# Sliding-window attention: turning the probabilities by VectorE's block transposes and a trip through DRAM, with a unit's scores moved forward

## The chip, the cores and the metric

The kernel runs on one core of a Trainium2 chip, as one launch. The metric is the device time of that launch in microseconds (us), the median of several runs. Everything is in float32. The core has five engines that work side by side, each through its own queue in order: TensorE (PE, matrix products; PEld is its loading of weights), VectorE (DVE), ScalarE (ACT), GpSimd (POOL) and SyncE (SP), which here only issues DMAs. Engines wait for each other by semaphores.

## The reference

1024 tokens (4 sequences of 256) of 512 features go through three residual steps: `x = x + 0.5 * ffn(layernorm(x))`, `x = x + attn(layernorm(x))`, and the first step again. `ffn` is a base product of 512x512 with a routed low-rank part (8 experts of rank 16, the two best for each token). `attn` is the part that the change touches:

```python
q = (x @ wq).reshape(B, S, 32, 128)        # 32 query heads
k = (x @ wk).reshape(B, S, 8, 128)         # 8 key/value heads, 4 query heads share one
v = (x @ wv).reshape(B, S, 8, 128)
q, k = rope(q, pos), rope(k, pos)
scores = einsum(qg, k) * 128 ** -0.5
allowed = (j <= i) & (j > i - 128)         # a window of 128 keys
attn = softmax(where(allowed, scores, neg))
out = einsum(attn, v) @ wo
```

## The kernel before, in words

Tokens are handled in two halves of 512 (two sequences each). After the first `ffn`, attention runs over 16 **groups**, one for each half `h` and key/value head `g`; `n` in the code is the number of a group, 1 to 16. A group has two **units**, one for each sequence `b`; there are 32 units.

The big products (queries, keys, values, output) use a 2x2 scheme with seven instead of eight block products, so many sums and differences of weights and activations run on GpSimd: `sum_weights` (wqs, wks, wvs), `sum_o_weights` (wos, four operations, each from the one before), and the sums of `outputs` (oTs). A group's `queries` are seven products, numbered in the code; after products 2, 5, 4 and 3 VectorE applies `rope` (one operation L484 and two L486 each, and an addition before it for 5, 4 and 3) and GpSimd adds the two parts into `qT` (L492).

A unit's attention is worked in blocks of 32 query positions (BLK), with four query heads side by side on the 128 partitions (32 positions x 4 heads). Queries of the first half of a sequence (4 blocks) see keys of the first half only; those of the second half see a window that spans both. The steps of a unit are:

- `scores` (L684): eight products on TensorE into PSUM (sa: the first four blocks; sb: the other four, two banks); VectorE adds the mask and takes maxima for sa (L696), and for sb puts the two ends of each window in place with a predicated copy (L714) and takes the maxima (L716).
- `exponentials` (L720): two small VectorE operations scale the maxima (L722, L723); ScalarE makes eight exponentials with their sums (L729) into `probs`, a single buffer for all units.
- `normalize` (L734): reciprocal on VectorE (L735), two multiplications of 128x512 on GpSimd (L738).
- `transposes` (L742): TensorE turns each of the eight 128x128 blocks of `probs` (L746), ScalarE copies the first four out of PSUM (L750), VectorE multiplies the other four by the masks `old` and `new` (L755), which split a window by the half that its keys are in.
- `values` (L761): one product oa for the first half, two that add up in ob (old keys, new keys), and two copies by ScalarE to `oT` (L771).
- `outputs` (L777): four sums on GpSimd and a list `late` of four steps, the output products y in the order (4), (1,6), (2,3), (7,5). They are not run at once but strewn between the next unit's work by `run(late, ...)`. The first, (4), reads the last of the four sums wos.

The order on TensorE, VectorE, ScalarE and GpSimd is the order of the program (`manual_schedule`), up to the last three units, where a scheduler orders TensorE and VectorE. In a group's first unit a string gives the order. Its letters are the query products 1 to 7, `y` a late output step, `n` normalize, `t` turn, `w` sum_o_weights, and some steps that only certain groups have (`k` `v` in the first group; `c` `d` `e` differences of tokens in group 7; `a` work of the last ffn near the end):

```python
order = {0: "1n6kv2754t3", 4: "1yn6a27cy5d4yte3yw"}[len(late)]
```

After it come the scores of the second unit, the values of the first, and the start of the next group's keys (odd `n`) or values (even `n`). The second unit runs the rest of those products, late steps, its own transposes, the scores of the next group's first unit, and its values. PSUM has four banks for products and four for scores and transposes. All DMAs are issued by SP, in one queue; the weights of a later group are loaded ahead.

Of the kernel before, what the change touches and what calls it, by code (L numbers as in the profile page):

```python
# [38 lines left out]
def macaron_kernel(  # L39
# [17 lines left out]
    const = ctx.enter_context(tc.tile_pool(name="const", bufs=1))  # L57
    sb = ctx.enter_context(tc.tile_pool(name="sb", bufs=2))
    ps = ctx.enter_context(tc.tile_pool(name="ps", bufs=2, space=bass.MemoryType.PSUM))

    def mm_bank(name):
        return ps.tile([P, 512], F32, tag="mm", bufs=4, name=name)
# [23 lines left out]
    nc.sync.dma_start(out=cos_sb, in_=cos[:, :S])  # L86
    sin_sb = const.tile([HD, S], F32, name="sin_sb")
    nc.sync.dma_start(out=sin_sb, in_=sin[:, :S])

    weights = {}  # L90

# [118 lines left out]
        return bass.AP(tensor=w.tensor, offset=w.offset, ap=[w.ap[0], [-BLK, 2], w.ap[2]])  # L210


    probs = const.tile([P, 2 * NB, P], F32, name="probs")
    for e in range(NB - 1):
        nc.gpsimd.memset(probs[:, e, (e + 1) * BLK :], 0.0)


    old = const.tile([P, NB, BLK], F32, name="old")
# [405 lines left out]
    def project_values(h, g):  # L624


        x, w = xs[h], weights["vs", h, g]
        dst = sb.tile([P, TPH, 2 * HD], F32, tag="v", name=f"v_{h}_{g}")
        vS[h, g] = dst
        banks = [mm_bank(f"v{n}_{h}_{g}").rearrange("p (b i f) -> p b i f", b=BPH, i=2) for n in range(2)]  # L630
        (c11, c12), (c21, c22) = ((bank[:, 0], bank[:, 1]) for bank in banks)
        (v11, v12), (v21, v22) = (
            (dst[:, :2, cols], dst[:, 2:, cols]) for cols in (slice(0, HD), slice(HD, 2 * HD))
        )
        p1c, u2, v1 = (
            temp(n, f"v_{h}_{g}")[:, :S].rearrange("p (i f) -> p i f", i=2) for n in ("p1c", "u2", "v1")
        )

        def product(n, bank, start=False):
            for i in range(2):  # L640
                for c in range(2):
                    nc.tensor.matmul(  # L642
                        bank[:, i, :], x[n - 1][:, c, ts(i, P)], w[n - 1][:, c, :],
                        start=(start and i == 0 and c == 0), stop=(c == 1), skip_group_check=True,
                    )

        def first():
            product(1, c11, True)
            nc.scalar.copy(p1c, c11)
            product(6, c22, True)  # L650

        def both():
            add(u2, c22, p1c)

        def second():
            product(5, c12)
            add(v1, c12, u2)
            product(7, c21)
            add(v22, c21, v1)

        def others():
            product(2, c11)
            product(4, c21)
            add(v21, c21, u2)
            product(3, c12)
            nc.scalar.copy(v11, c11)
            add(v12, c12, u2)

        return first, both, second, others

# [10 lines left out]
        nc.scalar.copy(vS[h, g][:, i, :], pv[:, : 2 * HD])  # L681


    def scores(h, g, b):  # L684
        o = b * S
        q, k = qT[h, g][:, b], kT[h, g]
# [7 lines left out]
        for e in range(NB):  # L694
            n = (e + 1) * BLK
            nc.vector.tensor_tensor_reduce(  # L696
                pr[:, e, :n], pa[:, e, :n], mask[:, P - n :], SM_SCALE, -3.4e38,
                ALU.add, ALU.max, mx[:, e : e + 1],
            )
        pairs = []  # L700
        for p in range(NB // 2):
            pb = score_bank(f"sb_{h}_{g}_{b}_{p}")
            for r in range(2):

                m = 2 * p + r
                at = r * P + m * BLK
                nc.tensor.matmul(  # L707
                    pb[:, at : at + P + BLK], q[:, NB + m],
                    k[:, o + m * BLK : o + m * BLK + P + BLK], start=True, stop=True,
                )  # L710
            w = picked(p)
            n = w.shape[-1]
            pb = pb.rearrange("p (r k) -> p r k", k=P)
            nc.vector.copy_predicated(pb[:, :2, :n], w, pb[:, 1:3, :n])  # L714
            pb = pb[:, :2, :]
            nc.vector.tensor_reduce(mx[:, NB + 2 * p : NB + 2 * p + 2], pb, AX.X, ALU.max)  # L716
            pairs.append(pb)
        return pr, mx, sm, pairs, f"{h}_{g}_{b}"

    def exponentials(pr, mx, sm, pairs, name):  # L720
        nm = sb.tile([P, 2 * NB], F32, tag="nm", bufs=3, name=f"nm_{name}")
        nc.vector.tensor_scalar(nm[:, :NB], mx[:, :NB], -1.0, None, ALU.mult)  # L722
        nc.vector.tensor_scalar(nm[:, NB:], mx[:, NB:], -SM_SCALE, None, ALU.mult)  # L723
        for n in range(2 * NB):
            keys_of = min(n + 1, NB) * BLK
            src, scale = (
                (pr[:, n, :], 1.0) if n < NB else (pairs[(n - NB) // 2][:, n % 2, :], SM_SCALE)
            )
            nc.scalar.activation(  # L729
                pr[:, n, :keys_of], src[:, :keys_of], AF.Exp, bias=nm[:, n : n + 1], scale=scale,  # L730
                accum_out=sm[:, n : n + 1],
            )

    def normalize(pr, sm):  # L734
        nc.vector.reciprocal(sm, sm)  # L735
        for n in range(0, 2 * NB, NB):
            w = pr[:, n : n + NB, :]
            nc.gpsimd.tensor_tensor(  # L738
                w, w, sm[:, n : n + NB].unsqueeze(2).to_broadcast([P, NB, P]), ALU.mult
            )  # L740

    def transposes(h, g, b, pr):  # L742
        def turn(n0, name):
            pt = ps.tile([P, NB, G, BLK], F32, tag="s", bufs=4, name=f"{name}_{h}_{g}_{b}")
            for e in range(NB):
                nc.tensor.transpose(pt[:, e, :, :], pr[:, n0 + e, :], ident)  # L746
            return pt

        p0 = sb.tile([P, NB, G, BLK], F32, tag="p0", bufs=1, name=f"p0_{h}_{g}_{b}")
        nc.scalar.copy(p0, turn(0, "t0"))  # L750
        pt = turn(NB, "t1")
        parts = []
        for n, w in enumerate((old, new)):
            part = sb.tile([P, NB, G, BLK], F32, tag=f"p1{n}", bufs=1, name=f"p1{n}_{h}_{g}_{b}")
            nc.vector.tensor_tensor(  # L755
                part, pt, w.unsqueeze(2).to_broadcast([P, NB, G, BLK]), ALU.mult
            )
            parts.append(part)
        return p0, parts

    def values(h, g, b, p0, p1):  # L761
        oT = sb.tile([HD, G, S], F32, tag="oT", bufs=4, name=f"oT_{h}_{g}_{b}")
        v = vS[h, g - g % 2]
        cols = ts(g % 2, HD)
        for i, parts in enumerate(([p0], p1)):
            po = mm_bank(f"o{'ab'[i]}_{h}_{g}_{b}")
            for n, part in enumerate(parts):
                nc.tensor.matmul(  # L768
                    po, v[:, 2 * b + n, cols], part, start=(n == 0), stop=(n == len(parts) - 1)
                )  # L770
            nc.scalar.copy(  # L771
                oT[:, :, ts(i, P)].rearrange("p j (e q) -> p e j q", e=NB),
                po.rearrange("p (e j q) -> p e j q", e=NB, j=G),
            )
        return oT

    def outputs(h, g, b, oT):  # L777
# [179 lines left out]
    last = units[-1]  # L957
    ahead = scores(*units[0])
    exponentials(*ahead)
    for u, (h, g, b) in enumerate(units):  # L960
        n = groups.index((h, g)) + 1
        left = len(units) - u
        if left == 3:
            in_order.close()
        if left < 4:
            normalize(ahead[0], ahead[2])
        fill(left, 0)
        if left == 1:
            nc.scalar.activation(root, eps, AF.Sqrt)
        parts = []  # L970

        def turn(at=(h, g, b), pr=ahead[0]):
            parts.extend(transposes(*at, pr))

        if b == 0 and n < len(groups):

            order = {0: "1n6kv2754t3", 4: "1yn6a27cy5d4yte3yw"}[len(late)]
            steps = queries(*groups[n], nc.vector.tensor_copy, ends)  # L980
            steps |= {
                "y": lambda: run(late, 1), "n": lambda: normalize(ahead[0], ahead[2]),
                "w": lambda: sum_o_weights(h, g), "v": lambda: project_v(0, 0, 2),
                "k": lambda: sum_weights("k", *groups[2]), "a": lambda: fill(left, 1),
                "t": turn, "c": None, "d": None, "e": None,
            }

            if g == NKV - 2 and h + 1 < NHALF:
# [6 lines left out]
        elif b == 1 and n + 1 < len(groups):  # L995
# [3 lines left out]
            if g == NKV - 2 and h + 1 < NHALF:  # L999
                more_tokens[4]()  # L1000
            second()
            normalize(ahead[0], ahead[2])
            if n == 2:
                for t in behind:
                    measure(t, "a")
            if n % 2 == 1 and (h, g) != groups[NKV]:
                sum_weights("v", *groups[n + 1])
            others()
            fill(left, 4)
            turned = [behind.popleft() for _ in range(2 if behind and n in (4, 6) else 0)]  # L1010
            for t in turned:
                scale(t, "a")
            if n % 2 == 0 and n + 2 < len(groups):
                sum_weights("k", *groups[n + 2])
# [2 lines left out]
            elif n % 2 == 0 and n + 2 < len(groups):  # L1017
                load_v(*groups[n + 2])
            run(late, len(late) - 1)
            for t in turned:  # L1020
                norm_attn(t, scaled=True)
        else:
            run(late, len(late))
            fill(left, 1)
        if b == 1 and n + 1 < len(groups):
# [12 lines left out]
        if b == 0 and 1 < n < len(groups):  # L1038
            load_o(*groups[n])
        if not parts:  # L1040
            turn()
        fill(left, 2)
        run(late, len(late) - 1)
        if left > 1:
            ahead = scores(*units[u + 1])

        combine = late.popleft() if g == NKV - 1 and b == 1 and left > 1 else None
# [3 lines left out]
        if u == 0:  # L1051
            project_v(0, 0, 3)
            load_v(*groups[2])
        oT = values(h, g, b, *parts)
        if b == 0 and n + 1 < len(groups):

            first, *begun = keys(*groups[n + 1]) if n % 2 == 1 else project_values(*groups[n])
            first()
        if left > 1:
            exponentials(*ahead)  # L1060
            if combine:
                combine()
            late.extend(outputs(h, g, b, oT))
# [73 lines left out]
```

## Time and profile before

| | |
|---|---|
| time, median of 3 runs | 765.95 us (765.70 to 766.31) |
| span of the profiled execution, first to last instruction | 764.3 us |
| mean granted TensorE clock | 0.999 of full speed |
| busy share of the span: PE, POOL, DVE, ACT | 99%, 71%, 73%, 28% |
| DMA, share of 16 engines | 18.7% |

The profile is of one execution; for that execution the page gives the span, and the times are those of the three runs, so what lies around the span is taken as the difference of the median and the span, 1.65 us. In a row of the timeline the first number is the start in us from the start of the span, the second the time from the first instruction's start to the last one's end; then engine, line, operation, output <- inputs, shapes, and how many instructions; brackets hold the idle time before it and what ended it. Products of 128x256 show up as two instructions each. Products overlap, so the price of a step on TensorE is the distance from its start to the start of what follows.

### The profile page before, as it was taken

The page shows a single profiled execution, that of the slowest core. Times are in us where ns is not written, and L with a number is a line of the kernel's source. Part 1 is how long each engine was busy: PE and PEld are TensorE (multiplying, and loading weights), DVE is VectorE, ACT ScalarE, POOL GpSimd, SP SyncE. Part 2 cuts the span into 40 slices and gives each one's busy share as a digit, 9 for nine tenths or more (in the row PEclk, how much of TensorE's full clock was granted, in tenths as well). Part 3 has the DMA queues.
Part 4 walks back from the last instruction along what each step waited for, and adds up shares of the span by engine and source line. Part 5 has one row for each costly group of instructions (what it writes and reads, how often), then busy time and mean ns, then how long its engine had stood idle before and what let it go on. Part 6 is the DMA issues. An engine that isn't in the chain of part 4 may idle for free.

```text
span 764.3 us, 11179 instructions
## 1 busy us (share of the span) xinstructions
PE 757.1 (99%) x3894; PEld 633.6 (83%) x3894; DVE 560.1 (73%) x1344; ACT 210.3 (28%) x749; POOL 541.6 (71%) x591
## 2 busy tenths in 40 slices
PE   8999999999999999999999999999999999999998
PEld 6877888888888888888888888888888888888866
DVE  5797885858675867668667867486867867595977
ACT  5421132422223130322222233213042222223331
POOL 6877775848767595769585788759575959865843
PEclk9999999999999999999999999999999999999999
DMA  9302111304030303112030303030301111010001
GB/s 318 123 1 83 52 59 30 109 1 138 1 111 28 111 28 97 42 57 83 20 118 1 129 9 111 28 111 29 107 31 56 56 49 63 1 56 28 2 27 56
DMA packets 29480, 48.97 MB, mean 64 GB/s; under 512 B 1136, under 2 KB 10352, under 8 KB 29424
## 3 DMA queue, kind: packets, MB, share of 16 engines
q1 hardware_dynamic: 29424, 48.26, 18.7%
q8 instruction: 31, 0.51, 0.3%
q14 instruction: 25, 0.20, 0.1%
HBM read 46.15 MB, written 2.10 MB: 63 GB/s over the span
## 4 chain that ended last, share of the span: by engine, by line
PE 96%; DVE 1%; DMA 1%; POOL 0%; SPq 0%; issue 0%; ACT 0%; DVEq 0%; ACTq 0%
PE q L533 25%; PE y L794 25%; PE ob L768 7%; PE k L590 6%; PE v L642 6%; PE sb L707 5%; PE sa L693 4%; PE oa L768 4%; PE t L746 4%; PE p_f L380 3%; PE po_f L380 2%; PE pa_f L344 2%; PE po_f L443 1%; DMA wb_sb<-in_w_base_dram 1%; PE po_f L360 1%; PE y L836 1%
## 5 line engine op out<-in xcount | busy, mean ns | idle before, releaser
L492 POOL TENSOR_TENSOR qT<-ra_q,rb_q 128x512 f32<-128x512 f32 x64 | 81.3, 1272 | 108.6 <-DVE rb_q L486 108.6
L486 DVE TENSOR_TENSOR rb_q<-q,sin_sb 64x512 f32<-64x512 f32 x128 | 88.0, 688 | 1.7
L750 ACT COPY p<-t 128x512 f32<-128x512 f32 x32 | 18.7, 586 | 211.7 <-PE t L746 211.7
L738 POOL TENSOR_TENSOR probs<-probs,sm 128x512 f32<-128x512 f32 x64 | 65.2, 1039 | 15.4 <-DVE sm L735 14.9
L794 PE MATMUL y<-wos,oT 128*128 128x256 f32 x248 | 63.7, 379 | 0.0
L794 PE MATMUL y<-wo,oT 128*128 128x256 f32 x248 | 63.7, 379 | 0.0
L794 PE MATMUL y<-wo,oTs 128*128 128x256 f32 x244 | 62.6, 379 | 0.0
L533 PE MATMUL q<-xs,wq 128*128 128x256 f32 x256 | 60.6, 379 | 0.2 <-DVE rb_k L486 0.2
L533 PE MATMUL q<-xa,wq 128*128 128x256 f32 x256 | 60.6, 379 | 0.0
L533 PE MATMUL q<-xs,wqs 128*128 128x256 f32 x256 | 60.5, 379 | 0.0
L768 PE MATMUL ob<-p,v 128*128 128x512 f32 x128 | 60.2, 592 | 0.0
L484 DVE TENSOR_TENSOR ra_q<-q,cos_sb 128x512 f32<-128x512 f32 x64 | 44.3, 691 | 20.4 <-PE q L533 14.8
L533 PEld LDWEIGHTS q<-xa,wq 128*128 128x128 f32 x256 | 48.4, 190 | 12.4 <-issue 6.2
L771 ACT COPY oT<-oa 128x512 f32<-128x512 f32 x32 | 18.7, 585 | 135.8 <-PE oa L768 135.8
L533 PEld LDWEIGHTS q<-xs,wq 128*128 128x128 f32 x256 | 48.6, 190 | 7.1 <-issue 0.5
L533 PEld LDWEIGHTS q<-xs,wqs 128*128 128x128 f32 x256 | 48.7, 190 | 6.6
L794 PEld LDWEIGHTS y<-wo,oT 128*128 128x128 f32 x248 | 46.6, 190 | 6.0
L794 PEld LDWEIGHTS y<-wo,oTs 128*128 128x128 f32 x244 | 46.4, 190 | 6.3
L794 PEld LDWEIGHTS y<-wos,oT 128*128 128x128 f32 x248 | 45.8, 190 | 5.3
L768 PEld LDWEIGHTS ob<-p,v 128*128 128x128 f32 x128 | 24.3, 190 | 30.6 <-issue 22.7
L729 ACT ACTIVATE probs<-probs,nm 128x32 f32<-128x32 f32 (+3 forms) x128 | 44.6, 351 | 11.4 <-DVE nm L722 6.0
L729 ACT ACTIVATE probs<-sb,nm 128x128 f32<-128x128 f32 x128 | 44.3, 353 | 0.0
(221 smaller groups left out, 1779.5 us busy)
## 6 DMA issues: line engine op xcount, KB each, us to landing
wq<-in_wq_dram SPq DMA_DIRECT2D x16, 1024.0 KB, 5.5
wo<-in_wo_dram SPq DMA_DIRECT2D x16, 1024.0 KB, 5.1
wk<-in_wk_dram SPq DMA_DIRECT2D x8, 512.0 KB, 3.4
wv<-in_wv_dram SPq DMA_DIRECT2D x8, 512.0 KB, 3.5
x<-in_x_dram SPq DMA_DIRECT2D x8, 256.0 KB, 6.1
out_dram<-x SPq DMA_DIRECT2D x7, 256.0 KB, 2.0
wb_sb<-in_w_base_dram SPq DMA_DIRECT2D x1, 1024.0 KB, 7.5
ar_sb<-in_w_ar_dram SPq DMA_DIRECT2D x1, 272.0 KB, 3.9
```

What stands on the lines that cost most here:

```text
L380: nc.tensor.matmul(bank[:, ts(i, D // 2)], lhs[j][m - 1][:, c, :], weights["bs"][m - 1][:, c, :], start=(m in (1, 5, 2, 4) and c == 0), st ...
L484: nc.vector.tensor_tensor(twice(a), twice(src), angle(cos_sb), ALU.mult)
L486: nc.vector.tensor_tensor(twice(b[o : o + half, :]), twice(src[i : i + half, :]), angle(sin_sb[o : o + half, :]), ALU.mult,)
L492: nc.gpsimd.tensor_tensor(dst, view(a), view(b), ALU.add)
L533: nc.tensor.matmul(bank[:, ts(j, S)], w[:, c, ts(j, HD)], x[:, c, :], start=(new and j == 0 and c == 0), stop=(c == 1), skip_group_check=True,
L590: nc.tensor.matmul(dst, w[n - 1][:, c, :], x[n - 1][:, c, :], start=(start and c == 0), stop=(c == 1), skip_group_check=True,)
L642: nc.tensor.matmul(bank[:, i, :], x[n - 1][:, c, ts(i, P)], w[n - 1][:, c, :], start=(start and i == 0 and c == 0), stop=(c == 1), skip_gr ...
L707: nc.tensor.matmul(pb[:, at : at + P + BLK], q[:, NB + m], k[:, o + m * BLK : o + m * BLK + P + BLK], start=True, stop=True,)
L729: nc.scalar.activation(pr[:, n, :keys_of], src[:, :keys_of], AF.Exp, bias=nm[:, n : n + 1], scale=scale, accum_out=sm[:, n : n + 1],)
L738: nc.gpsimd.tensor_tensor(w, w, sm[:, n : n + NB].unsqueeze(2).to_broadcast([P, NB, P]), ALU.mult)
L768: nc.tensor.matmul(po, v[:, 2 * b + n, cols], part, start=(n == 0), stop=(n == len(parts) - 1))
L794: nc.tensor.matmul(py[:, ts(i, D // 2)], lhs[n - 1][:, c, :], weights["os", h, g][n - 1][:, c, :], start=(i == 0 and c == 0), stop=(c == 1 ...
```

## The change

The eight transposes of a unit leave TensorE. `probs` gets another layout (partition, block of 32 keys, block of 32 queries, key), VectorE turns 32x32 blocks in place (two operations of 128x512, `turn_blocks`), SP stores the result to a DRAM buffer `kept` in two DMAs of 256 KB, and four DMAs (`fetch`, one for each block of keys, 32 partitions each) load it into `turned`, which then has keys on partitions. ScalarE's copy of the first half is gone. Instead of two masked copies only one is made (`split`): the second half's product is `turned` x old values + `part` x (new values - old values), and `difference` makes that difference of the values in place, once for each pair of heads. The scale of the scores is folded into the rope tables at the start (two GpSimd operations), and maxima are taken negated, so the two small operations in `exponentials` are gone.

The order string changes too. `T` turns the first unit's blocks, stores and fetches; `t` is now `split`; `S` is the scores and exponentials of the group's second unit, now in front of query product 4; `N` is its normalize and `U` its block transposes and stores, after `t` and ahead of `w`. The second unit's fetch follows the first unit's values.

```diff
+    root_scale = SM_SCALE ** 0.5
+    for table in (cos_sb, sin_sb):
+        nc.gpsimd.tensor_scalar(table, table, root_scale, None, ALU.mult)
...
-    probs = const.tile([P, 2 * NB, P], F32, name="probs")
+    probs = const.tile([P, NB, 2 * NB, BLK], F32, name="probs")
+    turned = const.tile([P, G, 2 * NB, BLK], F32, name="turned")
...
             add(v12, c12, u2)
+            difference(h, g)
...
-                pr[:, e, :n], pa[:, e, :n], mask[:, P - n :], SM_SCALE, -3.4e38,
-                ALU.add, ALU.max, mx[:, e : e + 1],
+                pr[:, : e + 1, e, :], blocks(pa[:, e, :n]), blocks(mask[:, P - n :]), -1.0, 3.4e38,
+                ALU.add, ALU.min, mx[:, e : e + 1],
...
-        nm = sb.tile([P, 2 * NB], F32, tag="nm", bufs=3, name=f"nm_{name}")
-        nc.vector.tensor_scalar(nm[:, :NB], mx[:, :NB], -1.0, None, ALU.mult)
-        nc.vector.tensor_scalar(nm[:, NB:], mx[:, NB:], -SM_SCALE, None, ALU.mult)
...
     def normalize(pr, sm):
         nc.vector.reciprocal(sm, sm)
-        for n in range(0, 2 * NB, NB):
-            w = pr[:, n : n + NB, :]
+        for c in range(0, NB, 2):
+            w = pr[:, c : c + 2]
...
-    def transposes(h, g, b, pr):
...
+    def turn_blocks(pr, name):
+
+        kept = dram.tile([P, NB, 2 * NB * BLK], F32, tag="kept", name=f"kept_{name}")
+        for c in range(0, NB, 2):
+            w = pr[:, c : c + 2].rearrange("p c n k -> p (c n k)")
+            nc.vector.transpose(w, w)
+            nc.sync.dma_start(
+                out=kept[:, c : c + 2, :], in_=pr[:, c : c + 2].rearrange("p c n k -> p c (n k)")
+            )
+        return kept.rearrange("(j k) c x -> k j c x", j=G)
+
+    def fetch(heads):
+        for c in range(NB):
+            nc.sync.dma_start(
+                out=turned[ts(c, BLK), :, c:, :].rearrange("p j n q -> p j (n q)"),
+                in_=heads[:, :, c, c * BLK :],
+            )
+
+    def split(h, g, b):
+        part = sb.tile([P, G, NB, BLK], F32, tag="part", bufs=1, name=f"part_{h}_{g}_{b}")
+        nc.vector.tensor_tensor(
+            part, turned[:, :, NB:, :], new.unsqueeze(1).to_broadcast([P, G, NB, BLK]), ALU.mult
+        )
+        return [turned[:, :, :NB, :]], [turned[:, :, NB:, :], part]
+
+    def difference(h, g, tiles=slice(None)):
+
+        pairs = vS[h, g].rearrange("p (b i) f -> p b i f", i=2)[:, tiles]
+        nc.vector.tensor_tensor(pairs[:, :, 1], pairs[:, :, 1], pairs[:, :, 0], ALU.subtract)
...
-            order = {0: "1n6kv2754t3", 4: "1yn6a27cy5d4yte3yw"}[len(late)]
+            order = {0: "1n6kTvD275t4S3NU", 4: "1yn6aT27cy5dS4ye3tNUyw"}[len(late)]
...
         oT = values(h, g, b, *parts)
+        if away:
+            turn()
...
         if left > 1:
-            exponentials(*ahead)
+            if not early:
+                exponentials(*ahead)
```

More of the change, by code (lines that the diff above doesn't have):

```diff
@@ L59, in macaron_kernel @@
     ps = ctx.enter_context(tc.tile_pool(name="ps", bufs=2, space=bass.MemoryType.PSUM))
+    dram = ctx.enter_context(tc.tile_pool(name="dram", bufs=2, space=bass.MemoryType.DRAM))
     def mm_bank(name):
@@ L210, in picked @@
         return bass.AP(tensor=w.tensor, offset=w.offset, ap=[w.ap[0], [-BLK, 2], w.ap[2]])
-    probs = const.tile([P, 2 * NB, P], F32, name="probs")
+    probs = const.tile([P, NB, 2 * NB, BLK], F32, name="probs")
+    turned = const.tile([P, G, 2 * NB, BLK], F32, name="turned")
     for e in range(NB - 1):
-        nc.gpsimd.memset(probs[:, e, (e + 1) * BLK :], 0.0)
+        nc.gpsimd.memset(probs[:, e + 1 :, e, :], 0.0)
+    for c in range(1, NB):
+        nc.gpsimd.memset(turned[ts(c, BLK), :, :c, :], 0.0)
     old = const.tile([P, NB, BLK], F32, name="old")
@@ L681, in project_v, with blocks @@
         nc.scalar.copy(vS[h, g][:, i, :], pv[:, : 2 * HD])
+    def blocks(t):
+        return t.rearrange("p (c k) -> p c k", k=BLK)
     def scores(h, g, b):
@@ L715, in scores @@
             pb = pb[:, :2, :]
-            nc.vector.tensor_reduce(mx[:, NB + 2 * p : NB + 2 * p + 2], pb, AX.X, ALU.max)
+            nc.vector.tensor_reduce(mx[:, NB + 2 * p : NB + 2 * p + 2], pb, AX.X, ALU.max, negate=True)
             pairs.append(pb)
@@ L720, in exponentials @@
     def exponentials(pr, mx, sm, pairs, name):
-        nm = sb.tile([P, 2 * NB], F32, tag="nm", bufs=3, name=f"nm_{name}")
-        nc.vector.tensor_scalar(nm[:, :NB], mx[:, :NB], -1.0, None, ALU.mult)
-        nc.vector.tensor_scalar(nm[:, NB:], mx[:, NB:], -SM_SCALE, None, ALU.mult)
         for n in range(2 * NB):
-            keys_of = min(n + 1, NB) * BLK
+            dst = pr[:, : min(n + 1, NB), n, :]
             src, scale = (
-                (pr[:, n, :], 1.0) if n < NB else (pairs[(n - NB) // 2][:, n % 2, :], SM_SCALE)
+                (dst, -1.0) if n < NB else (blocks(pairs[(n - NB) // 2][:, n % 2, :]), 1.0)
             )
             nc.scalar.activation(
-                pr[:, n, :keys_of], src[:, :keys_of], AF.Exp, bias=nm[:, n : n + 1], scale=scale,
-                accum_out=sm[:, n : n + 1],
+                dst, src, AF.Exp, bias=mx[:, n : n + 1], scale=scale, accum_out=sm[:, n : n + 1]
             )
@@ L735, in normalize @@
         nc.vector.reciprocal(sm, sm)
-        for n in range(0, 2 * NB, NB):
-            w = pr[:, n : n + NB, :]
+        for c in range(0, NB, 2):
+            w = pr[:, c : c + 2]
             nc.gpsimd.tensor_tensor(
-                w, w, sm[:, n : n + NB].unsqueeze(2).to_broadcast([P, NB, P]), ALU.mult
+                w, w, sm.unsqueeze(1).unsqueeze(3).to_broadcast([P, 2, 2 * NB, BLK]), ALU.mult
             )
-    def transposes(h, g, b, pr):
[L743 to L756, printed above, removed]
-            )
-            parts.append(part)
-        return p0, parts
@@ L764, in values @@
         cols = ts(g % 2, HD)
-        for i, parts in enumerate(([p0], p1)):
+        for i, parts in enumerate((p0, p1)):
             po = mm_bank(f"o{'ab'[i]}_{h}_{g}_{b}")
@@ L770, in values @@
                 )
[L771 to L774, printed above, removed]
+            nc.scalar.copy(oT[:, :, ts(i, P)], po.rearrange("p (j q) -> p j q", j=G))
         return oT
@@ L959, in macaron_kernel, with once @@
     exponentials(*ahead)
+    done, away = set(), []
+    def once(what, act):
+        if what not in done:
+            done.add(what)
+            act()
     for u, (h, g, b) in enumerate(units):
@@ L964, in macaron_kernel, with level, turn_ahead, turn @@
             in_order.close()
+        def level():
+            once(f"n{ahead[-1]}", lambda: normalize(ahead[0], ahead[2]))
+        def turn_ahead():
+            once(f"t{ahead[-1]}", lambda: away.append(turn_blocks(ahead[0], ahead[-1])))
+        def turn():
+            turn_ahead()
+            if away:
+                fetch(away.pop())
         if left < 4:
-            normalize(ahead[0], ahead[2])
+            level()
         fill(left, 0)
@@ L970, in macaron_kernel, with look_ahead, part @@
         parts = []
-        def turn(at=(h, g, b), pr=ahead[0]):
-            parts.extend(transposes(*at, pr))
+        def look_ahead(at=u + 1):
+            nonlocal ahead
+            ahead = scores(*units[at])
+            exponentials(*ahead)
+        def part(at=(h, g, b)):
+            parts.extend(split(*at))
         if b == 0 and n < len(groups):
-            order = {0: "1n6kv2754t3", 4: "1yn6a27cy5d4yte3yw"}[len(late)]
+            order = {0: "1n6kTvD275t4S3NU", 4: "1yn6aT27cy5dS4ye3tNUyw"}[len(late)]
             steps = queries(*groups[n], nc.vector.tensor_copy, ends)
             steps |= {
-                "y": lambda: run(late, 1), "n": lambda: normalize(ahead[0], ahead[2]),
+                "y": lambda: run(late, 1), "n": level, "N": level, "U": turn_ahead, "S": look_ahead,
+                "D": lambda: difference(0, 0, slice(1)),
                 "w": lambda: sum_o_weights(h, g), "v": lambda: project_v(0, 0, 2),
                 "k": lambda: sum_weights("k", *groups[2]), "a": lambda: fill(left, 1),
-                "t": turn, "c": None, "d": None, "e": None,
+                "T": turn, "t": part, "c": None, "d": None, "e": None,
             }
@@ L1001, in macaron_kernel @@
             second()
-            normalize(ahead[0], ahead[2])
+            level()
             if n == 2:
@@ L1008, in macaron_kernel @@
             others()
+            turn()
             fill(left, 4)
-            turned = [behind.popleft() for _ in range(2 if behind and n in (4, 6) else 0)]
-            for t in turned:
+            shifted = [behind.popleft() for _ in range(2 if behind and n in (4, 6) else 0)]
+            for t in shifted:
                 scale(t, "a")
@@ L1019, in macaron_kernel @@
             run(late, len(late) - 1)
-            for t in turned:
+            for t in shifted:
                 norm_attn(t, scaled=True)
         else:
+            turn()
             run(late, len(late))
@@ L1040, in macaron_kernel @@
         if not parts:
-            turn()
+            part()
         fill(left, 2)
         run(late, len(late) - 1)
-        if left > 1:
+        early = ahead[-1] == "{}_{}_{}".format(*units[u + 1]) if left > 1 else False
+        if left > 1 and not early:
             ahead = scores(*units[u + 1])
@@ L1054, in macaron_kernel @@
         oT = values(h, g, b, *parts)
+        if away:
+            turn()
+        if u == 0:
+            difference(0, 0, slice(1, 2))
         if b == 0 and n + 1 < len(groups):
@@ L1059, in macaron_kernel @@
         if left > 1:
-            exponentials(*ahead)
+            if not early:
+                exponentials(*ahead)
             if combine:
```

## The prediction

> **What bounds the kernel now.** First the page's busy shares and its chain of waits:
>
> ```profile
> PE 757.1 (99%) x3894; PEld 633.6 (83%) x3894; DVE 560.1 (73%) x1344; ACT 210.3 (28%) x749; POOL 541.6 (71%) x591
> PE 96%; DVE 1%; DMA 1%; POOL 0%; SPq 0%; issue 0%; ACT 0%; DVEq 0%; ACTq 0%
> ```
>
> TensorE is the bound, so whatever leaves it is gain, and whatever makes it wait is loss. Next the timeline of TensorE over one steady group, the fourth (each pass of two units is a group):
>
> ```profile
> 209.07 1.89 PE L533 MATMUL q<-xs,wqs 128*128 128x256 f32 x8
> 214.25 1.04 PE L746 MATMUL t<-ident,probs 128*128 128x128 f32 x8
> 215.12 1.89 PE L533 MATMUL q<-xa,wqs 128*128 128x256 f32 x8
> 218.58 1.05 PE L693 MATMUL sa<-kT,qT 128*128 128x32 f32 x8
> 221.42 1.88 PE L768 MATMUL ob<-p,v 128*128 128x512 f32 x4
> 223.14 1.05 PE L642 MATMUL v<-wv,xa 128*128 128x128 f32 x8
> 224.92 1.03 PE L794 MATMUL y<-wos,oT 128*128 128x256 f32 x4
> ```
>
> The distance between starts is the price: the eight transposes of a unit hold TensorE for 215.12 - 214.25 = 0.87 us. Last, the same stretch on VectorE and GpSimd:
>
> ```profile
> 211.00 0.70 DVE L512 TENSOR_TENSOR q<-q,v_q 128x512 f32<-128x512 f32 x1 [1.04 <-PE q L533]
> 213.93 0.70 DVE L512 TENSOR_TENSOR q<-q,u_q 128x512 f32<-128x512 f32 x1
> 216.86 0.69 DVE L811 TENSOR_TENSOR x<-y,x 128x512 f32<-128x512 f32 x1
> 217.47 0.68 DVE L755 TENSOR_TENSOR p<-t,old 128x512 f32<-128x512 f32 x1
> 218.66 0.69 DVE L512 TENSOR_TENSOR q<-q,u_q 128x512 f32<-128x512 f32 x1
> 221.58 0.69 DVE L804 TENSOR_TENSOR z<-y,z 128x512 f32<-128x512 f32 x1
> 222.19 0.18 DVE L696 CUSTOM_DVE_ANT_0 probs<-sa,mask 128x32 f32<-128x32 f32 x1
> 224.29 0.42 DVE L722 TENSOR_SCALAR nm<-mx 128x4 f32<-128x4 f32 x1
> 218.14 1.27 POOL L126 TENSOR_TENSOR wos<-wo 128x512 f32<-128x512 f32 x1
> 222.19 1.27 POOL L126 TENSOR_TENSOR wos<-wo,wos 128x512 f32<-128x512 f32 x1
> 223.41 1.27 POOL L492 TENSOR_TENSOR qT<-ra_q,rb_q 128x512 f32<-128x512 f32 x1
> 228.38 2.04 POOL L738 TENSOR_TENSOR probs<-probs,sm 128x512 f32<-128x512 f32 x2 [0.71 <-DVE sm L735]
> ```
>
> VectorE is only 73% busy over the span, but from 211.00 to 224.7 it has no gap. And GpSimd finishes the four sums wos at 223.46, 1.5 us before the product y<-wos at 224.92 that reads the last of them. Those two facts decide this change.
>
> **Removed.** 32 units x 0.87 us = 27.8 us of TensorE, all on the chain. Off the chain: ScalarE's copy L750 (0.59 us), one of VectorE's two products L755 and its two L722/L723 operations, in every unit.
>
> **The round trip.** Two VectorE transposes of 128x512, two stores of 256 KB, four loads of at most 128 KB. No row shows a block transpose: nearest are VectorE's other 128x512 operations, 0.68 to 0.70; I take 0.69, bounds 0.3 to 1.4. [...] For a store the nearest row is the output's 256 KB, 2.0 us to landing; for loads, 3.4 (512 KB) in steady state, 8.1 in the queue at the start. First unit of a group: normalized at +6.0 us from the group's first product, transposes end at +6.65, stores land at +9, loads at +14, wanted at +23: 9 us to spare, and 16 us in all, about what the dearest rows (8.1 + 8.1) come to. Second unit: transposes end at +26, loads land by about +33, wanted at +42. On SP's queue only the loads of wq and wo come between, and both are used 20 us later. So the DMA costs 0, at worst about 1 us a unit. VectorE's first pair of transposes delays the rope of q2 by 0.4 us, and its next wait for TensorE (1.04 us ahead of 211.00) takes that up.
>
> **The second unit's scores, moved ahead of q4.** This is where I see the loss. On TensorE they only change places. But the queues of VectorE and GpSimd now read, after q5:
> VectorE: rope of q5, scores, rope of q4, x, rope of q3, part, reciprocal. GpSimd: second unit's normalization, then the four wos, then qT, then oTs.
> VectorE's row, from the rows above: add and rope of q5 213.93 - 211.00 = 2.93; scores 224.29 - 222.19 = 2.10; add and rope of q4 2.93; x 0.61; add and rope of q3 221.58 - 218.66 = 2.92; part 0.59 (pitch of L755); reciprocal 0.20. Sum 12.28, with TensorE never the later one, so the reciprocal ends at 223.28. GpSimd normalizes from 223.35 to 225.35 (2.0 us, L738), then sums wos in 223.41 - 218.14 = 5.27 us: done at 230.62, and y<-wos starts near 230.7.
> TensorE, without t and with the scores in front, would be at the part product of ob at 221.41 but part ends at 223.08: it waits 1.7 us. It does ob and v and waits again from 225.8 to 230.7, **4.9 us**. y<-wos is at 230.7 instead of 224.92, 5.78 later; the second unit's absent transposes give 0.87 back: **+4.9 us a group**. What follows y<-wos keeps its distances: the k ropes end about 10 us after it as before, oTs is made in time, exponentials follow the values.
> Eleven groups (2 to 6, 8, 9, 11 to 14): 54. Group 7 has a sum xs on VectorE in that row: 5.8. Group 10: GpSimd still has the additions L830, oTs and wvs ahead of the normalization (in the profile that ends 14 us into the group, harmless as t comes at +14.7); now VectorE's transposes wait for it, with the rope of q2 and v1 queued behind them and q4 behind v1. VectorE reaches q5's add at +19.1 instead of +11.4: 4.9 + 7.6 = 12.5. Group 15 has 3.5 us of other products in front of y: 3.3. Group 1 has neither wos nor y in its loop; it waits for the first loads: 0.7. Two table scalings at the start (GpSimd, nearest row 0.30 for 128x128): 0.5. In the last two units the transposes saved and the round trip cancel: 0. Together **77 us**.
>
> **Other edits.** The difference of values is eight VectorE operations (0.69 or two halves) where it has gaps of 0.4 to 1.2 us; without that cover, 5 us. Part now reads two SBUF inputs; L504, of that kind, took 1.30 beside GpSimd and 0.68 otherwise. GpSimd is idle then, so 0, at most 0.6 a group. The second pair of transposes runs beside wos: 0 to 1.3 us a group. One-input operations of VectorE in SBUF beside GpSimd are the nearest rows (L723 once 1.20 instead of 0.15), and there VectorE was held up while GpSimd's additions kept their 1.27; nothing waits for the second pair, so I take 0. The strided exponentials have 4 us to spare.
>
> **The clock.** No idle time of TensorE in this profile is long, but two rows frame one of 4.9 us:
>
> ```profile
> 1.56 4.26 PE L173 MATMUL idle<-ident 128*128 128x128 f32 x20 [1.56 <-POOL ident masks.py:199]
> 10.73 3.70 PE L360 MATMUL po_f<-wb_sb,xn_f 128*128 128x512 f32 x8 [0.76 <-DMA wb_sb<-in_w_base_dram]
> ```
>
> Out of rest, twenty transposes came every 0.21 us, not every 0.11: 2.0 us lost. After 0.76 us of waiting nothing was lost. The price of my fourteen stalls lies between 0 and 14 x 2.0 = 28 us (a gain is excluded, waiting speeds nothing up); the stalls lie between the two rows, so I take half, 14.
> [...]
>
> **Sum.** The span of 764.3 becomes 764.3 + 77 + 14 = 855.3. The times shown (median 765.95) lie 1.65 above that span: 857.
>
> **Rivals.**
> 1. Faster: the waits are covered and only the removal counts, 765.95 - 27.8 + 0.5 = **739**. For: 27.8 us do leave an engine that is 99% busy, and GpSimd is idle 29% of the time. Against: it turns on one point, that y<-wos is not more than 1.7 us late per group. For that wos must end by 225.8, so the reciprocal by 218.5; VectorE has 4.8 us more of rope and scores ahead of it than that allows. Chance 0.06; 0.01 more for no change and 0.01 for a small gain.
> 2. Same stalls, clock untouched: **843**. For: each stall is short of the start's rest. Chance 0.26.
> 3. Every stall cools TensorE (871), and GpSimd's sums are held up by VectorE's transposes (14 x 1.3 more, 889): 0.17.
> 4. The round trip through DRAM is not hidden, by 1 to 2 us in each unit because loads of 640 to 1024 bytes per run are slow: 857 + 32 to 64, from **889**. Against: 9 us to spare at ordinary prices. Chance 0.04.
> My own case has 0.45.
>
> **Numbers.** The range takes in cases 2, mine and most of 3: down to 826, where a stall is 1.2 us smaller than I reckon in each of 14 groups and the clock is untouched, up to 886. About 0.15 lies outside. Faster by over 0.2% (about what a measurement of this kernel tells from no change): 0.07, within 0.2% 0.01, slower 0.92.
>
> **What would show it.** In the profile after: TensorE's share near 90%; the list of waits led, for TensorE, by y waiting for wos (about 4.9 us, 14 times) and ob for part (1.7); the turned loads landing some 9 us before part; the reciprocal of the second unit 12.3 us after q5's add; idle GpSimd ahead of the second normalization; low granted clock after some stalls. I am wrong if y<-wos does not wait, or if TensorE waits for a load.

## The result, and the profile after

The changed kernel takes 882.41 us (881.58 to 883.01) where the kernel before took 765.88 on the same chip: a ratio of 1.152, 95% interval 1.150 to 1.153. The profiled execution has a span of 879.8 us, 115.5 more than before, and a mean granted clock of 0.955 instead of 0.999.

The busy shares (busy us, share of the span, instructions), the shares of the chain of waits and the row of the granted clock, from the page of the kernel after:

```profile
PE 771.5 (88%) x3638; PEld 627.9 (71%) x3638; DVE 583.0 (66%) x1321; ACT 191.9 (22%) x717; POOL 550.2 (63%) x596
PEclk9999998999999899999999998999999898998999
PE 52%; DVE 20%; POOL 19%; issue 9%; ACT 0%; DVEq 0%; POOLq 0%
```

TensorE was 96% of the chain and is now 52%: the end is set in turn by TensorE, VectorE's row and GpSimd's. TensorE's waits, from the list of waits (total us, times, longest):

```profile
PE y L810 <- POOL wos L131: 64.2, 15, 4.7
PE ob L787 <- DVE part L770: 22.1, 14, 3.1
PE q L541 <- DVE rb_q L494: 9.5, 3, 8.4
```

The first two are the two waits that were forecast (of the fifteen before y, fourteen lie in the groups 2 to 15; the last one, of 0.5 us, is in the tail); 8.4 of the third is group 10. TensorE over one steady group, the fifth (first product at 267.09):

```profile
267.09 1.89 PE L541 MATMUL q<-xa,wq 128*128 128x256 f32 x8
288.06 1.02 PE L787 MATMUL ob<-turned,v 128*128 128x512 f32 x2
290.68 1.13 PE L787 MATMUL ob<-part,v 128*128 128x512 f32 x2 [1.60 <-DVE part L770]
292.50 1.03 PE L598 MATMUL k<-xs,wks 128*128 128x256 f32 x4
298.22 2.08 PE L810 MATMUL y<-wos,oT 128*128 128x256 f32 x4 [4.69 <-POOL wos L131]
300.09 1.91 PE L598 MATMUL k<-xs,wks 128*128 128x256 f32 x4
303.14 1.03 PE L598 MATMUL k<-xa,wk 128*128 128x256 f32 x4
```

The second column tells a second story: after the wait of 4.69 us four matmuls of 128x256 take 2.08 and 1.91 us instead of 1.03. TensorE came back at half its clock: the trace has it granted at 0.50 from 295.93 on. The work that it waited for, on VectorE and GpSimd:

```profile
278.51 0.70 DVE L520 TENSOR_TENSOR q<-q,v_q 128x512 f32<-128x512 f32 x1 [1.04 <-PE q L541]
289.93 0.69 DVE L770 TENSOR_TENSOR part<-turned,new 128x512 f32<-128x512 f32 x1
290.54 0.20 DVE L743 RECIPROCAL sm<-sm 128x8 f32<-128x8 f32 x1
290.87 2.05 POOL L746 TENSOR_TENSOR probs<-probs,sm 128x512 f32<-128x512 f32 x2 [3.15 <-issue]
292.88 1.27 POOL L131 TENSOR_TENSOR wos<-wo 128x512 f32<-128x512 f32 x1
296.90 1.26 POOL L131 TENSOR_TENSOR wos<-wo,wos 128x512 f32<-128x512 f32 x1
```

GpSimd sits idle for 3.15 us in front of the second normalization. The row puts that down to issue, but the normalization reads the reciprocal, which ends at 290.74, and it starts 0.13 us later; the four sums wos stand behind it. The last one ends at 298.16, and y starts at 298.22.

### The profile page after: what moved, and what is told of

Its sections match the earlier page's. It is cut to its first block, busy times and chain, and to the rows that moved or that the text cites. A ratio compares the mean times of both kernels' runs of the same rounds, so it can differ in the third digit from the quotient of the medians.

```text
span 879.8 us, 11047 instructions
## 1 busy us (share of the span) xinstructions
PE 771.5 (88%) x3638; PEld 627.9 (71%) x3638; DVE 583.0 (66%) x1321; ACT 191.9 (22%) x717; POOL 550.2 (63%) x596
## 4 chain that ended last, share of the span: by engine, by line
PE 52%; DVE 20%; POOL 19%; issue 9%; ACT 0%; DVEq 0%; POOLq 0%
PE y L810 15%; PE q L541 15%; POOL wos L131 6%; DVE rb_q L494 5%; PE k L598 4%; PE v L650 4%; POOL probs L746 4%; DVE q L520 3%; PE ob L787 3%; POOL wo L131 2%; PE sb L719 2%; DVE ra_q L492 2%; PE sa L705 2%; PE oa L787 1%; DVE mx L728 1%
## 5 line engine op out<-in xcount | busy, mean ns | idle before, releaser
L810 PE MATMUL y<-wos,oT 128*128 128x256 f32 x248 | 77.8, 443 | 64.2 <-POOL wos L131 64.2
L810 PEld LDWEIGHTS y<-wos,oT 128*128 128x128 f32 x248 | 51.6, 218 | 75.6 <-POOL wos L131 69.0
L827 DVE TENSOR_TENSOR x<-y,x 128x256 f32<-128x256 f32 (+1 forms) x62 | 34.4, 554 | 79.1 <-PE y L810 78.6
L738 ACT ACTIVATE probs<-probs,mx 128x32 f32<-128x32 f32 (+3 forms) x128 | 44.7, 351 | 166.7 <-DVE mx L708 166.6
L755 DVE STREAM_TRANSPOSE probs<-probs 128x512 f32<-128x512 f32 x64 | 45.3, 710 | 44.0 <-POOL probs L746 43.5
L541 PE MATMUL q<-xs,wqs 128*128 128x256 f32 x256 | 62.9, 390 | 9.5 <-DVE rb_q L494 9.5
L787 PE MATMUL ob<-part,v 128*128 128x512 f32 x64 | 34.2, 617 | 22.1 <-DVE part L770 22.1
L810 PEld LDWEIGHTS y<-wo,oTs 128*128 128x128 f32 x244 | 46.4, 190 | 6.3
L126 POOL TENSOR_TENSOR oTs<-oT 128x256 f32<-128x256 f32 x31 | 22.7, 731 | 42.9 <-ACT oT L790 42.9
```

What stands on the lines that cost most here:

```text
L541: nc.tensor.matmul(bank[:, ts(j, S)], w[:, c, ts(j, HD)], x[:, c, :], start=(new and j == 0 and c == 0), stop=(c == 1), skip_group_check=True,
L738: nc.scalar.activation(dst, src, AF.Exp, bias=mx[:, n : n + 1], scale=scale, accum_out=sm[:, n : n + 1])
L755: nc.vector.transpose(w, w)
L787: nc.tensor.matmul(po, v[:, 2 * b + n, cols], part, start=(n == 0), stop=(n == len(parts) - 1))
L810: nc.tensor.matmul(py[:, ts(i, D // 2)], lhs[n - 1][:, c, :], weights["os", h, g][n - 1][:, c, :], start=(i == 0 and c == 0), stop=(c == 1 ...
```

## The clock, window by window

The trace holds the granted clock over time. It has sixteen slow stretches ahead of the span's end (one more begins 0.2 us before it), all at 0.50. Each is one, two or three times 3.413 us long, and all begin on one grid of 3.413 us (for example at 149.16, 200.36, 248.15 and 295.93 us, which is 15, 14 and 14 steps apart). So the waits of this trace are best read on that grid. Windows of the kernel after: stretch, its length, TensorE's busy us and instructions, granted clock in that stretch, DMA share, GB/s:

```profile
237.91:241.32 3.41, 1.81 (x5) 1.00 0.54 204
241.32:244.73 3.41, 2.58 (x18) 1.00 0.47 180
244.73:248.15 3.42, 0.00 (x0) 1.00 0.63 199
248.15:251.56 3.41, 3.02 (x10) 0.50 0.03 7
251.56:254.97 3.41, 3.41 (x32) 1.00 0.00 0
...
289.11:292.52 3.41, 1.84 (x7) 1.00 0.80 286
292.52:295.93 3.41, 1.01 (x5) 1.00 0.44 156
295.93:299.35 3.42, 1.13 (x3) 0.50 0.54 122
299.35:302.76 3.41, 3.41 (x10) 0.50 0.00 0
302.76:306.17 3.41, 3.41 (x18) 1.00 0.00 0
```

In the fourth group the wait before y fills a whole window (0.00 busy), and the next window runs at half clock. In the fifth it falls across a boundary: a window with 1.01 us of work is followed by half clock, and after the next, with 1.13 us of work, half clock stays for a second one. The waits of 1.6 us before ob leave 1.81 us of work or more in their window, and the clock stays at 1.00. Over the whole trace the sixteen windows ahead of half clock held 0.00 to 1.34 us of work, and no window at full clock with 1.59 us or more was followed by it. All fourteen waits before y in the groups were followed by a slow stretch; for seven of them the window ahead of it held no work at all.

Laying TensorE's busy time over the slow stretches gives what they cost: 62.2 us of work at half clock, where it takes twice as long (2.08 and 1.91 us for 1.03 above), so **31.1 us lost**: 1.7 after the wait of 3.1 us before ob in group 7, 3.1 after the 8.4 us in group 10, and 1.9 on average after the fourteen waits before y.

The 115.5 us are then: 27.8 us of transposes gone, 31.1 lost to the clock, and the rest, 112.2, is waiting with the restarts after it, or 84.4 net of the transposes.

## The experiments

**1. The scores at their old place.** The turn by VectorE and DRAM stays.

```diff
-order = {0: "1n6kTvD275t4S3NU", 4: "1yn6aT27cy5dS4ye3tNUyw"}
+order = {0: "1n6kTvD2754t3", 4: "1yn6aT27cy5d4yte3yw"}
```

> The turn by VectorE and DRAM stays; the second unit's scores, normalization and turn go back to where they stood before. Theory (the place of the scores is the whole loss): y waits for wos and ob for part no more than 0.5 us each, the granted clock is 0.99 or more, and the 27.8 us of transposes are gained, less up to 2 us in some seven groups where the second unit's turn now stands behind the two ropes of the keys: 740 to 756 us. Rival (the turn itself costs: block transposes, the trip through DRAM, the two SBUF inputs of part): it stays above 850 us. In between, near 800 us, both have a share.

Measured: 821.24 us, 1.072 of the kernel before (1.070 to 1.073), clock 0.973. Neither theory: the time lies between the two, and the waits at y for wos are gone, those at ob for part down to 2.7 us in all, but a new one has come. The list of waits, then VectorE and TensorE at the end of a key group (the second unit's transposes and its product oa):

```profile
PE oa L787 <- DMA turned<-kept: 37.3, 12, 4.4
...
200.52 0.43 DVE L520 TENSOR_TENSOR k<-k,u_k 128x256 f32<-128x256 f32 x1
203.19 1.30 DVE L755 STREAM_TRANSPOSE probs<-probs 128x512 f32<-128x512 f32 x2
210.21 2.04 PE L787 MATMUL oa<-turned,v 128*128 128x512 f32 x2 [4.37 <-DMA turned<-kept]
```

From the first transpose to the loaded data the trip takes 6.8 us (203.19 to some 210). The scores at their old place leave the second unit too little room for it: oa waits up to 4.4 us in key groups and about 1.3 in some value groups, and the clock goes with it (19.9 us lost). So the loss is not just a matter of where the scores stand. The move of the scores is what hides the second unit's trip, and it is paid for at wos.

**2. wos ahead of the second normalization.**

```diff
-"1yn6aT27cy5dS4ye3tNUyw"
+"1yn6aT27cy5dS4ye3twNUy"
```

> As changed, but wos is summed ahead of the second normalization (w in front of N and U). Theory (GpSimd's queue: wos stands behind a normalization that waits for VectorE): wos ends 7 us earlier against the group's first product, y waits less than 0.5 us instead of 4.65; ob still waits 1.6 us for part. 882 less 14 x 4.65 less the 31 us of the slow clock gives 786 us; VectorE's transposes now wait some 4 us longer for their normalization, and if the additions behind them hold up the next key or value product by 3 us in 14 groups, 830 us. Rival (wos is late for another reason, such as its own sources): y waits as before, 870 to 883 us.

Measured: 816.36 us, 1.066 (1.064 to 1.068), clock 0.989. Its list of waits:

```profile
PE ob L787 <- DVE part L770: 26.2, 14, 4.0
PE k L598 <- DVE u_k L520: 10.5, 7, 2.2
PE q L541 <- DVE rb_q L494: 9.5, 3, 8.4
PE v L650 <- DVE u_v L520: 9.1, 7, 1.5
...
PE y L810 <- POOL wos L131: 0.5, 1, 0.5
```

The wait for wos fell from 64.2 to 0.5 us by exchanging two steps in GpSimd's queue: what made y late was the normalization in front of wos. The wait for part stayed, and part of the feared wait came, 1.5 us before a key or value product in ten of the groups and 0.9 in two more, so that the time lies between the 786 and the 830 us: VectorE's transposes now wait 3.4 us for their normalization, with the additions queued behind them.

**3. TensorE kept at work during the wait.** 40 transposes of the identity in front of y<-wos, from the second group on.

```diff
             both()
+            if n > 1:
+                for i in range(40):
+                    nc.tensor.transpose(idle[:, i % NB, :], ident, ident)
```

> As changed, with 40 transposes of the identity (0.108 us each, 4.3 us) on TensorE in front of y<-wos in every group from the second on, so that it waits no more than 0.4 us there; y starts no earlier. Theory (the half clock after a stall costs 31 us in all): the clock stays near 1.0 but for group 10, and 882 falls to 852 to 860 us. Rival (the slow clock hides in the chain of VectorE and GpSimd and costs nothing): 882 us with a granted clock near 1.0. Second rival (such transposes do not count as work for the clock): the clock stays at 0.955 and the time at 880 us or above.

Measured: 862.59 us, 1.126 (1.124 to 1.127), clock 0.986, which is 2.6 us above what was expected. In the eleventh group:

```profile
584.10 4.53 PE L1041 MATMUL idle<-ident 128*128 128x128 f32 x40
589.00 1.13 PE L810 MATMUL y<-wos,oT 128*128 128x256 f32 x4 [0.37 <-POOL wos L131]
589.97 1.03 PE L598 MATMUL k<-xs,wks 128*128 128x256 f32 x4
```

y still comes when wos is done, but the products behind it run at full clock (1.00 granted from 589 to 593 us; in the changed kernel 0.50 behind the same y), and useless work made the kernel 20 us faster. Both rivals fall: the time came down from 882 us, so the slow clock was on the path, and with these transposes in the waits the clock was 0.986 and not 0.955. What slow clock remains costs 8.7 us by the same reckoning as above: 7.0 in groups 10, 15 and 7, where the filler does not reach, and 1.7 after a wait of 2.2 us before a key product ahead of the second group. That wait was in the changed kernel too (2.17 us, at 106.61), but there it left 1.59 us of work in its window, and the clock stayed at 1.00. So 22.4 us of clock were won back, and some 4 given back elsewhere; where was not traced. From y to y of the next group the eleventh now takes 46.4 us (41.1 before, 47.9 after).

**4. The move alone, without the turn.** The kernel before, with TensorE's transposes.

```diff
-order = {0: "1n6kv2754t3", 4: "1yn6a27cy5d4yte3yw"}
+order = {0: "1n6kv2754t3", 4: "1yn6a27cy5dtS4ye3Nyw"}
 ...   (and the steps S and N, as the changed kernel has them)
```

> The kernel before, transposes on TensorE, with only the scores of the second unit in front of query product 4, its normalization in front of wos, and the first unit's transposes put ahead of the scores since probs is a single buffer. Theory (the place alone makes the loss): VectorE's row to the reciprocal is 2.93 + 1.3 + 2.5 + 2.93 + 0.61 + 2.92 + 0.2 = 13.4 us after q5's add, y<-wos is about 7 us late in 14 groups and the clock is lost for 2 us after each: 866 to 895 us. Rival (the turn by VectorE and DRAM is what costs): under 790 us.

Measured: 895.38 us, 1.168 (1.167 to 1.170), the upper end of what was expected, clock 0.941, with this wait on top:

```profile
PE y L794 <- POOL wos L126: 87.9, 14, 7.6
```

The move alone costs 129 us, 35.6 of them by the clock. TensorE waits 6.5 us in a steady group before y, about as much as the 1.6 and 4.7 us of the changed kernel together, but there 1.7 us of transposes come off in every group.

**5. A longer trip.** Every unit's transposed probabilities are stored twice.

```diff
+        for c in range(0, NB, 2):
+            nc.sync.dma_start(out=kept[:, c : c + 2, :], in_=...)   # the same two stores again
```

> As changed, but every unit's transposed probabilities are stored a second time before they are loaded (two more stores of 256 KB per unit, about 2 us more on the trip). Theory (the trip is hidden, with 6 to 10 us to spare, in the 30 units ahead of the tail): 880 to 888 us, the excess from the last two units, and no wait of TensorE for a load in the groups. Rival (the trip is on the path): 30 x 2 us more, above 930 us.

Measured: 890.09 us, 2 above what was expected. In the profile the steady groups are as long as without the stores (the fourth: 49.7 us from y to the next group's y in both, the tenth 47.8), and no wait for a load stands in the list. The profiled execution is 8.5 us longer than that of the changed kernel (the median 7.7): 2.4 us before the second group's y, 1.3 from there to the fifteenth group's, and 4.8 in the last two units. The trip is hidden in the changed kernel, but for those two units.

**6. to 10. Towards a version that keeps both.** If the trip needs the scores early, and wos and part suffer from the queues that this makes, the queues can be set in another order. Five attempts, one after the other:

```diff
 # old_early: scores at the old place, the second unit's turn ahead of the additions of its keys or values
             level()
+            turn()
             others()
-            turn()
 # new_order: scores early; part ahead of them, two output steps earlier, wos right after the last of them,
 #            the second normalization last, its turn as in old_early
-"1yn6aT27cy5dS4ye3tNUyw"
+"1yn6aT27cy5dtySyw4e3N"
 # new_order_b: the same, but the output steps stay where they were
+"1yn6aT27cy5dtS4ye3ywN"
 # all three, in group 10 only
+"1yn6a27cy5dT4ye3ytw"
```

> The scores at their old place, and the second unit's turn, stores and loads directly behind its normalization, ahead of the last key or value additions and ropes; in group 10 the first unit's turn stands behind q5 and its part last. Theory (with the scores at the old place the trip of about 6.7 us from transposes to part is only late because VectorE reaches the transposes 3.8 us after they could start): oa's wait for the loads falls from 4.2 to under 1 us in key groups and from 1.3 to 0 in value groups, the clock is 0.99 or more: 750 to 768 us. Rival (the trip itself is too long for that place, or VectorE's additions behind it now hold up TensorE by as much): oa or the key products wait 3 us or more in half the groups, over 795 us.

> The scores stay in front of q4, but part stands ahead of them, two output steps move up, wos is summed directly after the last of them and ahead of GpSimd's qT of q4, the second normalization comes last and its turn after the additions of the next unit; group 10 as in the other kernel. Theory (only VectorE's and GpSimd's queues made y and ob wait): wos ends near +22 us in the group, y at +24.4 does not wait, ob does not wait, nor does oa: 743 to 762 us, below the kernel before. Rival (VectorE's row of 12 us is the limit wherever GpSimd's work stands): TensorE waits 3 us or more a group for a rope or an addition, the clock falls, 800 us or more.

> As the kernel with the new order, but the output steps stay where they are, so that wos can only start after the last of them and qT of q4: part ahead of the scores, wos ahead of the second normalization, turn after the additions. wos then ends at +26 us where y is wanted at +24.4. Theory: ob no longer waits, y waits 1 to 2 us in 13 groups, no key or value product waits for VectorE, clock 0.99 or more: 757 to 775 us. Rival as for the new order: 800 us or more.

Measured: 782.76 us (ratio 1.019 to 1.026), 772.55 (1.006 to 1.011) and 804.36 (1.050 to 1.054). All three lie above what was expected, by 15, 11 and 29 us, and 10 to 13 us of it has one cause: the order that I gave group 10 puts its turn so late that oa waits 6.8 to 7.0 us for the loads, and 1.5 to 3 us again in the next unit, with 2 to 4 us of clock. In new_order_b the wait that it was built to show, wos behind the last output steps, came as expected: 23.1 us in 14 times. What was not expected is that half clock follows it: 10.6 us of clock in all, at a mean granted clock of 0.985 in the profiled execution. Its time lies in the rival's range, but not for the rival's reason, as no wait for a rope is longer than 0.7 us; the profiled execution took 798.74 us, so 5.6 us of the median lie in no trace. In old_early oa's wait outside group 10 fell to 3.4 us in all, and q waits 8 us for ropes. In new_order the two waits of the changed kernel are gone in the steady groups (y for wos 3.2 us in all, ob for part 1.3).

The next two kernels mend the dear groups of new_order. The first sums group 10's leftovers behind its normalization or on VectorE, and moves the sums of tokens of group 7; the second gives group 7 the order of the kernel before, and puts VectorE's additions of group 9 behind the scores.

```diff
 # tuned
-"1yn6aT27cy5dtySyw4e3N"            (and the order of group 10)
+"1ynx6aT27cy5tySywd43eN"           x, in group 10: the last two additions into x and wvs, on GpSimd
-    add_sums(h - 1, b, nc.gpsimd, slice(-2))
+    add_sums(h - 1, b, nc.vector, slice(-2))
 # tuned_b
+if g == NKV - 2 and h + 1 < NHALF:
+    order = "1yn6aT27cy5d4yte3yw"
 # and add_sums(h - 1, b, nc.vector, slice(-2)) moved behind the scores
```

> The new order, with its two dear groups mended: in group 10 the first unit is turned in its usual place, two of GpSimd's additions into x and the sums wvs follow the normalization, and the other additions go to VectorE; in group 7 the sums of tokens stand behind wos and behind the last query product. Theory (the 7 us that the new order lies above the span before come from group 10, +8.6 and +3.2 us, and group 7, +4.9): the wait of 7 us for the loads and the 2.7 us for wos go, and the time is 754 to 762 us, below the kernel before. Rival (the additions are due at those places and only move the wait): 766 to 775 us.

> As the tuned kernel, but group 7 keeps the order of the kernel before (scores at their old place, sums of tokens where they were), and in group 9 VectorE's additions stand behind the scores instead of ahead of part. Theory (what was left over the span before were 6.0 and 1.0 us in group 7, where a gain of 1.7 was due, and 4.5 us ahead of group 10, where 0.9 was due): both waits go, 754 to 760 us, below the kernel before by 0.8 to 1.6%. Rival (a wait moves on once more): 763 us or above.

Measured: tuned 767.34 us, 1.0005 to 1.0023 of the kernel before, not faster. The rival was right there: group 10 lost its wait, but the additions on VectorE made ob wait 3.4 us for part just ahead of it, and in group 7 a key product waited 5.7 us for a sum of tokens. tuned_b: **756.87 us, 0.988 of the kernel before (0.986 to 0.989)**, 14% less than the changed kernel. Its shares and its longest wait:

```profile
PE 734.5 (97%) x3638; PEld 606.1 (80%) x3638; DVE 590.0 (78%) x1325; ACT 191.6 (25%) x717; POOL 557.2 (74%) x592
PE q L541 <- DVE rb_q L494: 6.4, 9, 0.9
```

No wait is longer than 1.5 us and the clock is 1.0. The span is 9.0 us shorter than before, of the 27.8 us that left TensorE. The rest went, as far as it was traced, into q waiting for ropes in every second group (6.4 us and restarts), the scores of group 7 at their old place, and some 4 us at the start and in the tail.

## Why the prediction was right, and where a term was mis-sized

The forecast was 857 us; 882.4 were measured. Its mechanism holds step by step. Of the 25 us of excess the clock makes 17 and the sum of the waits 7. Both terms erred to the same side, and the time lies only 3.6 us below the upper end of the range, 886: that it lies inside is owed to the range, which took in most of rival 3, not to the sum.

- **VectorE's row.** 12.28 us from q5's addition to the end of the reciprocal; measured 290.74 - 278.51 = 12.23. From the group's first product to y 31.1 us were forecast, and 298.22 - 267.09 = 31.13 measured.
- **The waits.** 1.7 us at ob, 4.9 at y; measured 1.60 and about 4.7 (3.1 each in group 7). Experiment 2 shows that y's is GpSimd's order, experiment 4 that it needs no turn by VectorE.
- **The block transposes.** I took 0.69 us; 64 took 0.71 on average.
- **The trip.** At cost 0 with 9 us to spare in the first unit. The last of the four loads is issued by 276.8 in the fifth group and the loads of 96 to 128 KB take 2.6 to 2.9 us, so they land near 279.6, and part runs at 289.93: 10 us. TensorE waits for a load once, for 0.3 us. Experiment 5 adds two stores to it at no cost in the steady groups. (The dearest rows of the queue at the start are not 8.1 us: the second load of wo, 1024 KB, took 12.5. Nothing in the sum rested on it.)
- **Part with two SBUF inputs.** At cost 0, at most 0.6: in the changed kernel a first unit's part takes 0.69, with GpSimd idle. The bound was real: a second unit's part (at 115.33), beside kT and a sum wqs, took 1.26 us.
- **The sum of the waits, 77 us; measured 84.4.** Read from y to the next group's y, without the clock's share, group 10's 12.5, group 15's 3.3 and group 7's 5.8 hold (12.3, 3.2 and 5.7). The eleven steady groups cost 61.3 and not 54: seven of them 5.0 to 5.2 each instead of 4.9, of which restarts after a wait, which were not in the sum, are at least a part (the first product after the wait at ob takes 1.13 us, not 1.02), and four more than that, by waits that I had not looked at: 2.2 us before a key product ahead of the second group's y, 0.55 for a rope ahead of the y of groups 3 and 13, and 0.7 for transposes pt_a ahead of the fifth group's y. Group 1, the start and the tail make 0.7 more than was forecast.
- **The clock, 14 us; measured 31.1.** This is the term that was mis-sized, and the step that failed is "the stalls lie between the two rows, so I take half". It priced a stall at half of 0 to 2.0 us; the average was 1.9. Half clock followed all fourteen stalls, and two other waits too. Seven of the fourteen had a window without work ahead of it; the windows of the other seven held 0.05 to 1.34 us. As windows with up to 1.34 us were followed by half clock, a stall of 4.7 us could hardly pass here, an estimate from these numbers: whatever its place on the grid of 3.413 us, it leaves some window with at most 1.1 us of work (two windows of 3.41 less 4.7, halved). So each stall cost nearly as much as the dearer of the two rows, and the half was a choice that neither row showed.

Of the rivals, the third had the clock right ("every stall cools", 871) and was wrong in its second half: GpSimd's sums of wos kept their 1.27 us beside VectorE's transposes. With the waits as measured and the clock untouched, the time would be about 851, where rival 2 said 843.

## What to carry over

An operation that is moved forward takes its queue with it: before moving it, write down for each engine what then stands behind it, down to work of another purpose (here the sums wos, behind a normalization that waits for VectorE). Waits of TensorE of 3 us and more cost more than their length here (the fourteen before y 1.9 us each on top, on average), so a few of them that come back in every group are worth breaking into shorter ones or filling. And a change that takes work off the bounding engine is not yet a gain: the 27.8 us were there all along, and a third of them could be kept only after the order of three queues had been written anew.

## What the hardware showed unexpectedly

- In the kernel after, half clock followed windows of 3.41 us in which TensorE had been busy for 0.00 to 1.34 us, and none with 1.59 us or more. Full clock came back after windows that were busy for 2.98 us or more, and not after one with 2.74 us.
- With 40 transposes of the identity (4.53 us) in the wait before the eleventh group's y the granted clock was 1.00 behind it, where the changed kernel had 0.50; over the profiled execution it was 0.986 and not 0.955, and the kernel was 20 us faster.
- Where part, with two SBUF inputs, ran beside GpSimd's additions in the kernel after, one or both took longer than the 0.69 and 1.27 us of most others: at 115.33 part took 1.26 us and the sum wqs that began beside it 1.71; at 213.23 part kept 0.68 us and the sum wqs took 1.74. Block transposes in place (one input) left GpSimd's sums wos at 1.27 to 1.28 us.
